# A two-layer graph network on one core: head 0's row sums split anew between TensorE, DMA and GpSimd, and a group's end copied in another order

## The chip, the cores and the metric

The kernel runs on one core of a Trainium2 chip. The metric is the device time of one execution in microseconds. Before the change it is 2827.12 us, the median of three runs (2824.92 to 2828.86). The engines are called TensorE (PE in the profile, PEld for its weight loads), VectorE (DVE), ScalarE (ACT), GpSimd (POOL) and SyncE (SP, which here only issues DMAs).

## The reference

Two layers, each in the form `x = x + layer(relu(layernorm(x)))`, over 4096 nodes with 512 features, all in float32. Layer 0 is a dense attention of one head. The change touches layer 1 alone, a graph attention with 8 heads of 64:

```python
data1 = (data @ W.T + b).reshape(N, H, D)            # N=4096, H=8, D=64
src = jnp.einsum('nhd,xhd->nh', data1, src_proj)
trg = jnp.einsum('nhd,xhd->nh', data1, trg_proj)
e = src.T[:, :, None] + trg.T[:, None, :]
e = jnp.where(e >= 0, e, 0.01 * e) + connectivity[None, :, :]
scores = jax.nn.softmax(e, axis=-1)
out = jnp.einsum('hnm,hmd->hnd', scores, data1.transpose(1, 0, 2))
```

Here `connectivity` is the matrix adj itself. For each head and each target row n, all 4096 sources m need a weight exp(leaky(src + trg) + adj), the weighted sum of the values, and the sum of the weights (the denominator).

## The kernel before, in words

**Work of layer 1.** The target rows come in 4 blocks of 1024 and the heads in 2 halves of 4, which makes 8 *groups*; a group walks over 32 *tiles* of 128 sources. So there are 256 steps. In each step the 128 sources lie on the partitions and the 1024 target rows in the free dimension, and four weight tiles of 128x1024, one per head (`pr[i, m, 0..3]`), are made and used.

**How the weights are made.** The exponential of the leaky sum is split into factors of the row, factors of the source and a maximum, so that one VectorE instruction makes a head's tile.
- ScalarE writes exp(adj) into PSUM (`exps`, L1085, one buffer, called `ex`). It writes exp(adj + a source's term) into SBUF (`last_exps`, L1095, `e3`).
- VectorE makes heads 3, 0, 1, 2 in this order (`weigh`, L1136 and L1133). Head 3's product takes `e3` and row factors, both in SBUF. The other three take `ex` from PSUM. `ex` can be written again when head 2's product has read it.
- Head 0 takes a relu of ScalarE first (`relus`, L1118). In every fourth tile (`BY_LOG`: 3, 7, ..., 31) head 0 goes another way: ScalarE writes a relu of the row terms (`logs`, L1101), GpSimd adds adj to it in two halves (`add_logs`, L1107), and ScalarE takes the exponential (L1115). VectorE then makes three products instead of four. The second half add is put behind head 3's product of the tile before, by an added dependency.

**What TensorE does** (`gather`). Per tile 16 value matmuls (L1171; 32 columns of weights, 512 columns moving) and 4 denominator matmuls (L1176, `dn<-pr,d_m`). Each matmul uses one of four 32-column strips of the array, so that four run side by side. Heads 1 and 2 get their denominators from those four matmuls. The denominators of heads 3 and 0 are gathered elsewhere:
- head 3: GpSimd adds each tile into one accumulator (`acc`, L1147, 128x1024);
- head 0: 24 tiles (`BY_DMA`) are added by accumulating DMAs, issued by GpSimd, into two accumulators in turn (L1154; tiles 0 and 1 are copied there, both at tile 1, L1152). The 8 other tiles (6, 10, 14, 18, 22, 26, 29, 31) go to TensorE as two further matmuls each (`dn<-pr,zo`), on strips 0 and 1 or 2 and 3 in turn (`side`).

In a group's last tile, TensorE sums the accumulators over the partitions by matmuls with a column of ones.

**A group's end.** In the last tile's step ScalarE copies the four value banks to SBUF (`os`, L1204). The denominators' bank (`dn`) is copied as `od` (L1210) in `finish`, after the next group's first step. The new group's tile 0 writes the same banks, so TensorE waits for these copies. `finish` runs in pieces, one at each step listed in `PARTS`: at step 1 products with `pick` (L1214), which bring the denominators to rows; at steps 2, 6, 10 and 14 two full-array transposes per row tile, behind the tile's matmuls (L1230); then scaling on ScalarE (L1257); at steps 5, 9, 13 and 17 a DMA from GpSimd that adds x (L1262); and at steps 8, 12, 16 and 18 the store from SyncE (L1260, L1265).

**Order of the work.** The order is written out by hand: each engine runs its instructions in the order of emission. In step s the functions of `stages` run for tiles ahead of s: loads 4 ahead, exponentials and products 1, factors 2, relus of the logs 4, TensorE 0. Then comes one piece of `finish`. Loads, broadcasts and stores share SyncE's queue; half adds, accumulations and their DMAs share GpSimd's. Buffers: `pr0` three, the other products two each, adj tiles four, `rl` two, `lg` one.

Of the kernel before, what the change touches and what calls it, by code (L numbers as in the profile page):

```python
# [15 lines left out]
P = 128  # L16
# [12 lines left out]
def kernel(  # L29
# [942 lines left out]
    zo = l1.tile([P, 3], FP, name="zo")  # L972

# [19 lines left out]

    PARTS = (0, 1, 2, 4, 5, 6, 8, 9, 10, 12, 13, 14, 16, 17, 18)
    BY_LOG = (3, 7, 11, 15, 19, 23, 27, 31)
    BY_DMA = [m for m in range(NT) if m not in (6, 10, 14, 18, 22, 26, 29, 31)]  # L1000
    after = mybir.DependencyInfo(mybir.DependencyClass.Sync, mybir.DependencyReason.DATA)

    with tc.tile_pool(name="p", bufs=2) as prp, tc.tile_pool(name="za", bufs=1) as zp0, tc.tile_pool(
# [17 lines left out]
        for t, val in ((d0_0, 0.0), (d0_m, 0.0), (zo[:, 0:2], 0.0), (zo[:, 2:3], 1.0)):  # L1021
            nc.gpsimd.memset(t, val)

        def tables():
# [26 lines left out]
        row = ident.rearrange("p (r s) -> p s r", s=Q)  # L1051
        nc.vector.tensor_copy(pick, row[:, 0:2, :])
        nc.vector.tensor_tensor(pick[:, 1, 0:HV], pick[:, 1, 0:HV], row[:, 2, HV:2 * HV], ALU.add)

        def zload(i, k):
            b, g = groups[i]
# [38 lines left out]
            nc.scalar.activation(x_, ra[i, m], AF.Exp, bias=ld_m[:, h // HG, m:m + 1])  # L1095
            e3[i, m] = x_

        def logs(i, m):
            if m in BY_LOG:
                r = rlp.tile([P, WL], FP, name="lg", bufs=1)  # L1100
                nc.scalar.activation(r, us[i], AF.Relu, bias=nlg_m[:, groups[i][1], m:m + 1], scale=-(1.0 - SLOPE))  # L1101
                rl[i, m] = r

        def add_logs(i, m, half, behind=None):
            if m in BY_LOG:
# [15 lines left out]
        def weigh(i, m, order=ORDER):  # L1121
            h = groups[i][1] * HG
            x_ = ex.pop((i, m))
            for k in order:
                if (i, m, k) in pr:
                    continue
                w = (prp if k else pr0p).tile([P, WL], FP, name=f"pr{k}")
                if k == 0 and (i, m) == (0, 0):
                    r = rlp.tile([P, WL], FP, name="rl")
                    nc.vector.tensor_scalar(r, zs_[0, 0], g_m[:, 0, 0:1], d_m[:, 0, 0:1], ALU.max, ALU.mult)  # L1130
                    nc.vector.tensor_tensor(w, r, x_, ALU.mult)
                elif k == 0:
                    nc.vector.scalar_tensor_tensor(w, rl.pop((i, m)), ngd_m[:, h // HG, m:m + 1], x_,  # L1133
                                                   op0=ALU.subtract, op1=ALU.mult)
                else:
                    p_ = nc.vector.scalar_tensor_tensor(w, zs_[i, k], g_m[:, h + k, m:m + 1],  # L1136
                                                        e3.pop((i, m)) if k == 3 else x_,
                                                        op0=ALU.max, op1=ALU.mult)
                    if k == 3:
                        add_logs(i, m + 1, 1, p_)  # L1140
                pr[i, m, k] = w
            w = pr[i, m, 3]
            if m == 1:
                acc[i, 3] = acp.tile([P, WL], FP, name="acc3", bufs=1)
                nc.gpsimd.tensor_tensor(acc[i, 3], pr[i, 0, 3], w, ALU.add)
            elif m > 1:
                nc.gpsimd.tensor_tensor(acc[i, 3], acc[i, 3], w, ALU.add)  # L1147
            add_logs(i, m + 2, 0)
            if m == 1:
                for n in range(2):  # L1150
                    acc[i, 0, n] = acp.tile([P, WL], FP, name=f"acc0{n}", bufs=1)
                    nc.gpsimd.dma_start(acc[i, 0, n], pr[i, n, 0])  # L1152
            elif m > 1 and m in BY_DMA:
                nc.gpsimd.dma_start(acc[i, 0, (len(BY_DMA) + BY_DMA.index(m)) % 2], pr[i, m, 0], accum_op=ALU.add)  # L1154

        def gather(i, m):
            b, g = groups[i]
# [2 lines left out]
                pv[i] = ([[p_v.tile([P, BL], FP, name=f"pv{c}{q}") for q in range(HV)] for c in range(2)],  # L1160
                         p_v.tile([P, BL], FP, name="dn"))
            v, dn = pv[i]
            by_pe = [u for u in range(NT) if u not in BY_DMA]
            side = sum(u < m for u in by_pe) % 2

            def values(c):
                for q in range(HV):
                    for r in (side, 1 - side):
                        k = ((3, 0), (1, 2))[c][r]
                        for c0 in range(0, D, Q):  # L1170
                            nc.tensor.matmul(v[c][q][r * D + c0:r * D + c0 + Q, :],  # L1171
                                             va[:, m, g * HG + k, c0:c0 + Q],
                                             pr[i, m, k][:, q * BL:(q + 1) * BL], start=(m == 0), stop=last)

            def den(r, w, src, q, **fl):
                nc.tensor.matmul(dn[r * Q:r * Q + w.shape[1], :], w, src[:, q * BL:(q + 1) * BL], **fl)  # L1176

            values(0)
            if last:
                for r, a in enumerate((acc[i, 0, 0], acc[i, 3])):  # L1180
                    for q in range(HV):
                        den(r * HV + q, zo[:, 1:3], a, q, start=False, stop=False)
                if m in by_pe:
                    for q in range(HV):
                        den(side * HV + q, zo[:, 1 - side:3], pr[i, m, 0], q, start=False, stop=False)
            values(1)
            for r in (side, 1 - side):
                for q in range(HV):
                    hk = g * 2 + r
                    den(r * HV + q, d0_m[:, hk, m, :] if m else d0_0[:, hk, :], pr[i, m, r + 1], q,  # L1190
                        start=(m == 0), stop=(last and r == 1))
            if m in by_pe and not last:
                for q in range(HV):
                    den(side * HV + q, zo[:, 1 - side:3], pr[i, m, 0], q, start=False, stop=False)
            if last:
                for q in range(HV):
                    den(q, zo[:, 1:3], acc[i, 0, 1], q, start=False, stop=True)
            for k in range(HG):
                pr.pop((i, m - 1, k), None)
            if last:  # L1200
                os_ = [[osp.tile([P, BL], FP, name=f"os{c}{q}") for q in range(HV)] for c in range(2)]
                for c in range(2):
                    for q in range(HV):
                        nc.scalar.copy(os_[c][q], v[c][q])  # L1204
                late[i] = os_, dn

        def denominators(i):
            os_, dn = late.pop(i)
            od = osp.tile([P, BL], FP, name="od")
            nc.scalar.copy(od, dn)  # L1210
            yield os_
            pd = p_t.tile([P, JT, 2, 4], FP, name="pt")
            for j in range(JT):
# [54 lines left out]
        def finish_last(i):  # L1268

            ys = [ep.tile([P, WT // 2, HG, D], FP, name="e") for _ in range(2)]  # L1270
            for n in range(2):
                nc.sync.dma_start(ys[n], part(x1, i, n * WT // 2, WT // 2))
            yield
            dens = denominators(i)
            os_ = next(dens)
            pts = []
# [68 lines left out]
        logs(0, 3)  # L1345
# [53 lines left out]
```

## Time and profile before

| | us |
|---|---|
| median of three runs | 2827.12 |
| profiled execution | 2827.62 |
| its span, first to last instruction | 2825.8 |
| layer 1, group 0 (1623.5 to 1771.2) | 147.7 |
| groups 1 to 6 | 150.0, 147.6, 148.1, 148.7, 147.5, 148.1 |
| group 7 and the kernel's end | 164.6 |

The profiled execution has 1.8 us around its span, and is 0.5 us over the median. A group is counted from the start of head 3's product of its tile 0. Layer 1 takes some 1200 us of the span. In a timeline a line has start, duration, engine, line and operation, what it writes and reads, and how many instructions it merges; brackets hold the engine's idle time before it and what ended that. A float32 matmul stands there as two instructions, so x8 is four matmuls.

### The profile page before, as it was taken

How to read it: one execution, taken by the hardware profiler on the slowest of the kernel's cores; microseconds unless marked ns; L12 is line 12 of the kernel's file. 1: busy time of each engine (PE TensorE's matmuls, PEld its weight loads, DVE VectorE, ACT ScalarE, POOL GpSimd, SP SyncE). 2: the span in 40 equal slices, each digit the busy share in tenths (PEclk: the TensorE clock that was granted, in tenths of full speed). 3: DMA queues.
4: the chain of work that ended last, by engine and by line, in shares of the span. 5: the costliest groups of instructions: out<-in, count | busy, mean ns of one | idle time of the engine just before them, and what ended most of it. 6: DMA issues, size and time to landing. Idle time of an engine off the chain costs nothing.

```text
span 2825.8 us, 46844 instructions
## 1 busy us (share of the span) xinstructions
PE 2757.8 (98%) x16843; PEld 1491.8 (53%) x16843; DVE 2508.6 (89%) x3425; ACT 1474.2 (52%) x2217; POOL 1397.6 (49%) x1178
## 2 busy tenths in 40 slices
PE   7999999998999999999999899999999999999998
PEld 4885444444888888888885323323232322232222
DVE  7877799898887888888886799999999999999998
ACT  2212233333123333433432188988788888888786
POOL 5323434444011010011106687887878787878786
PEclk9999999999999999999999999999999999999999
DMA  5637898987999999898877379989999898989896
GB/s 178 178 96 265 266 338 295 309 293 232 192 191 212 205 228 242 223 234 225 216 193 186 101 198 242 241 211 247 223 244 221 239 223 238 227 242 219 212 224 168
DMA packets 535992, 629.86 MB, mean 223 GB/s; under 512 B 292152, under 2 KB 346456, under 8 KB 535760
## 3 DMA queue, kind: packets, MB, share of 16 engines
q1 hardware_dynamic: 461920, 415.87, 49.6%
q0 software_dynamic: 71824, 207.07, 33.6%
q10 hardware_dynamic: 2016, 3.93, 0.4%
q8 instruction: 132, 2.16, 0.3%
q14 instruction: 100, 0.82, 0.1%
HBM read 404.23 MB, written 107.15 MB: 181 GB/s over the span
## 4 chain that ended last, share of the span: by engine, by line
PE 65%; DVE 13%; DMA 6%; issue 5%; ACT 4%; POOL 3%; SPq 2%; DVEq 0%; POOLq 0%; ACTq 0%
PE po L729 22%; PE pv L1171 15%; PE pe L525 12%; DVE pr L1136 8%; PE bank L267 6%; PE dn L1176 5%; PE po L863 4%; DMA acc<-pr 3%; SPq L656 2%; ACT e L1095 2%; DVE pr L1133 1%; POOL acc L1147 1%; DMA et<-er_d 1%; DVE mk L514 1%; DMA a<-in_adj_t_dram 1%
## 5 line engine op out<-in xcount | busy, mean ns | idle before, releaser
L1171 PE MATMUL pv<-pr,sup 128*32 128x512 f32 x8192 | 986.3, 594 | 13.8 <-POOL d L1342 10.2
L1147 POOL TENSOR_TENSOR acc<-acc,pr 128x1024 f32<-128x1024 f32 x240 | 576.5, 2402 | 146.9 <-DVE pr L1136 145.3
L1136 DVE SCALAR_TENSOR_TENSOR pr<-z,g_m,ex 128x1024 f32<-128x1024 f32 x512 | 630.4, 1270 | 2.9 <-ACT ex L1085 1.6
L1171 PEld LDWEIGHTS pv<-pr,sup 128*32 128x32 f32 x8192 | 282.6, 110 | 611.9 <-issue 547.1
L525 PE MATMUL pe<-he_t,he_t 128*128 128x512 f32 x896 | 387.9, 594 | 0.0
L690 ACT ACTIVATE d<-d 128x1024 f32<-128x1024 f32 x126 | 133.1, 1056 | 444.3 <-DVE d L682 237.9
L1136 DVE SCALAR_TENSOR_TENSOR pr<-z,g_m,e 128x1024 f32<-128x1024 f32 x256 | 345.2, 1348 | 3.2 <-PE pv L1171 3.2
L1085 ACT ACTIVATE ex<-e 128x1024 f32<-128x1024 f32 x256 | 263.3, 1029 | 144.8 <-DVE pr L1136 142.9
L1176 PE MATMUL dn<-pr,d_m 128*2 128x512 f32 x1984 | 318.5, 592 | 0.0
L1095 ACT ACTIVATE e<-e,ld_m 128x1024 f32<-128x1024 f32 x256 | 291.3, 1138 | 0.0
L525 PEld LDWEIGHTS pe<-he_t,he_t 128*128 128x128 f32 x896 | 169.8, 191 | 209.3 <-issue 193.7
L729 PE MATMUL po<-he_t,at 128*128 128x256 f32 x1024 | 263.8, 380 | 5.5 <-ACT he_t L740 5.5
L729 PE MATMUL po<-sup,u 128*128 128x256 f32 x1024 | 263.3, 380 | 0.0
L729 PE MATMUL po<-sup,at 128*128 128x256 f32 x1024 | 245.3, 383 | 8.3 <-DVE at L700 7.3
L1133 DVE SCALAR_TENSOR_TENSOR pr<-rl,ngd_m,ex 128x1024 f32<-128x1024 f32 x191 | 242.6, 1270 | 8.2 <-ACT ex L1085 8.2
L1118 ACT ACTIVATE rl<-z,ngd_m,d_m 128x1024 f32<-128x1024 f32 x191 | 234.7, 1229 | 0.0
L816 POOL DMA_DIRECT2D he_t<-he_t x56 | 48.9, 958 | 359.3 <-ACT he_t L732 304.3
L700 DVE TENSOR_TENSOR at<-d,a 128x1024 f32<-128x1024 f32 x126 | 154.0, 1223 | 77.2 <-PE po L729 45.8
L729 PEld LDWEIGHTS po<-sup,at 128*128 128x128 f32 x1024 | 196.3, 192 | 36.4 <-DVE at L700 8.1
L729 PEld LDWEIGHTS po<-he_t,at 128*128 128x128 f32 x1024 | 195.0, 191 | 32.4 <-issue 5.9
L729 PEld LDWEIGHTS po<-sup,u 128*128 128x128 f32 x1024 | 194.2, 190 | 26.2
L530 POOL DMA_DIRECT2D er_d<-mk x136 | 74.5, 548 | 237.8 <-DVE rm L527 226.4
(268 smaller groups left out, 3831.7 us busy)
## 6 DMA issues: line engine op xcount, KB each, us to landing
e<-in_adj_t_dram SPq DMA_DIRECT2D x256, 512.0 KB, 6.0
acc<-pr POOLq DMA_DIRECT2D x192, 512.0 KB, 6.2
a<-in_adj_t_dram SPq DMA_DIRECT2D x126, 512.0 KB, 5.2
ac<-in_adj_t_dram SPq DMA_DIRECT2D x124, 256.0 KB, 5.3
ar<-in_adj_dram SPq DMA_DIRECT2D x120, 256.0 KB, 5.0
ec_d<-mc POOLq DMA_DIRECT2D x120, 256.0 KB, 5.0
er_d<-mk POOLq DMA_DIRECT2D x112, 256.0 KB, 4.6
et<-er_d SPq DMA_DIRECT2D x448, 64.0 KB, 4.1
```

What stands on the lines that cost most here:

```text
L267: nc.tensor.matmul(acc[:, j, :], w, m, start=(k == 0), stop=(k == KC // 2 - 1))
L525: nc.tensor.matmul(pe[:, :w], he_t[i][:, k, (t % TB) * P:(t % TB + 1) * P], he_t[j][:, k, BL - w:], start=(k == 0), stop=(k == KC - 1))
L700: nc.vector.tensor_tensor(w, d, aj.pop((n, q)), ALU.mult)
L729: nc.tensor.matmul(acc[:, j, :], A[:, j * P:(j + 1) * P], B, start=(first_ and j == 0), stop=last, skip_group_check=True)
L1085: nc.scalar.activation(x_, ra.pop((i, m)), AF.Exp)
L1095: nc.scalar.activation(x_, ra[i, m], AF.Exp, bias=ld_m[:, h // HG, m:m + 1])
L1118: nc.scalar.activation(r, zs_[i, 0], AF.Relu, bias=ngd_m[:, h // HG, m:m + 1], scale=d_m[:, h, m:m + 1])
L1133: nc.vector.scalar_tensor_tensor(w, rl.pop((i, m)), ngd_m[:, h // HG, m:m + 1], x_, op0=ALU.subtract, op1=ALU.mult)
L1136: p_ = nc.vector.scalar_tensor_tensor(w, zs_[i, k], g_m[:, h + k, m:m + 1], e3.pop((i, m)) if k == 3 else x_, op0=ALU.max, op1=ALU.mult)
L1147: nc.gpsimd.tensor_tensor(acc[i, 3], acc[i, 3], w, ALU.add)
L1171: nc.tensor.matmul(v[c][q][r * D + c0:r * D + c0 + Q, :], va[:, m, g * HG + k, c0:c0 + Q], pr[i, m, k][:, q * BL:(q + 1) * BL], start=(m = ...
L1176: nc.tensor.matmul(dn[r * Q:r * Q + w.shape[1], :], w, src[:, q * BL:(q + 1) * BL], **fl)
```

## The change

In layer 1:
- **Head 0's sums.** Tiles 4, 8, ..., 28 (`BY_HALF`) are split: TensorE takes the first 512 target rows by one matmul, on strip 0, 1, 2, 3 in turn, and GpSimd adds the other 512 into a third accumulator `acc02`. Tile 31 goes to TensorE as two matmuls on strips 2 and 3. The other 24 tiles go by DMA: 6, 10, 14, 18, 22, 26 and 29 do now, and 4, 8, ..., 28 no longer. In the last tile there is one matmul more, for `acc02`.
- **Order of strips.** The matmuls of a tile start on the strip behind the last extra one (`cols`), instead of on one of two sides. `pick` adds three more rows for the new places, and `zo` has four columns.
- **Tile 0 at once.** The copies of tiles 0 and 1 into the accumulators are issued each at its own tile.
- **The first log.** The relu for tile 3 is made 5 tiles ahead instead of 4 (`early_logs`); the others stay.
- **A group's end.** In the last step only the first two value banks are copied. The other two and `dn` are copied in the next group's step 0 (`rest`), behind the exponential of tile 1. `od` is now a buffer of the pool of output tiles; its own is gone, and `acc02` takes as much.
- **PARTS.** The last store of a finished group is issued at step 21, not 18.

```diff
-    PARTS = (0, 1, 2, 4, 5, 6, 8, 9, 10, 12, 13, 14, 16, 17, 18)
+    PARTS = (0, 1, 2, 4, 5, 6, 8, 9, 10, 12, 13, 14, 16, 17, 21)
     BY_LOG = (3, 7, 11, 15, 19, 23, 27, 31)
-    BY_DMA = [m for m in range(NT) if m not in (6, 10, 14, 18, 22, 26, 29, 31)]
+    BY_HALF = (4, 8, 12, 16, 20, 24, 28)
+    BY_DMA = [m for m in range(NT - 1) if m not in BY_HALF]
...
+        for c in range(1, 4):
+            nc.vector.tensor_tensor(pick[:, 1, 0:1], pick[:, 1, 0:1], row[:, 3, c:c + 1], ALU.add)
...
-        def logs(i, m):
-            if m in BY_LOG:
+        def logs(i, m, early=False):
+            if m in BY_LOG and early == (m == BY_LOG[0]):
...
-            if m == 1:
-                for n in range(2):
-                    acc[i, 0, n] = acp.tile([P, WL], FP, name=f"acc0{n}", bufs=1)
-                    nc.gpsimd.dma_start(acc[i, 0, n], pr[i, n, 0])
-            elif m > 1 and m in BY_DMA:
+            if m < 2:
+                acc[i, 0, m] = acp.tile([P, WL], FP, name=f"acc0{m}", bufs=1)
+                nc.gpsimd.dma_start(acc[i, 0, m], pr[i, m, 0])
+            elif m in BY_DMA:
                 nc.gpsimd.dma_start(acc[i, 0, (len(BY_DMA) + BY_DMA.index(m)) % 2], pr[i, m, 0], accum_op=ALU.add)
+            if m == BY_HALF[0]:
+                acc[i, 0, 2] = acp.tile([P, BL], FP, name="acc02", bufs=1)
+                nc.gpsimd.tensor_copy(acc[i, 0, 2], pr[i, m, 0][:, BL:])
+            elif m in BY_HALF:
+                nc.gpsimd.tensor_tensor(acc[i, 0, 2], acc[i, 0, 2], pr[i, m, 0][:, BL:], ALU.add)
...
-            by_pe = [u for u in range(NT) if u not in BY_DMA]
-            side = sum(u < m for u in by_pe) % 2
+            n = sum(u < m for u in BY_HALF) % 4
+            cols = [(n + c) % 4 for c in range(4)]
...
+                for q in range(HV):
+                    ones(q, 1, halves(acc[i, 0, 0])[q])
+                for q in range(HV):
+                    ones(HV + q, 1, halves(acc[i, 3])[q])
+                ones(1, 1, acc[i, 0, 2])
+                for q in range(HV):
+                    ones(HV + q, 2, halves(pr[i, m, 0])[q])
             values(1)
...
+            if m in BY_HALF:
+                ones(n, 3 if n else 1, halves(pr[i, m, 0])[0])
...
-                for c in range(2):
-                    for q in range(HV):
-                        nc.scalar.copy(os_[c][q], v[c][q])
-                late[i] = os_, dn
+                for q in range(HV):
+                    nc.scalar.copy(os_[0][q], v[0][q])
+                late[i] = os_, v[1], dn
+
+        def rest(i, m):
+            if i and m == 0:
+                copy_rest(i - 1)
+
+        def copy_rest(i):
+            os_, v, dn = late[i]
+            for q in range(HV):
+                nc.scalar.copy(os_[1][q], v[q])
+            od = iop.tile([P, BL], FP, name="o")
+            nc.scalar.copy(od, dn)
+            late[i] = os_, od
...
-        stages = ((load, 4), (exps, 1), (weigh, 1), (factors, 2), (logs, 4), (scale, 2), (gather, 0))
+        stages = ((load, 4), (exps, 1), (rest, 0), (weigh, 1), (factors, 2), (logs, 4), (early_logs, 5), (scale, 2), (gather, 0))
```

More of the change, by code (lines that the diff above doesn't have):

```diff
@@ L1162, in gather @@
             v, dn = pv[i]
[L1163 to L1164 removed]
+            n = sum(u < m for u in BY_HALF) % 4
+            cols = [(n + c) % 4 for c in range(4)]
             def values(c):
                 for q in range(HV):
[L1168 removed]
+                    for col in cols:
+                        r, c0 = col // 2, col % 2 * Q
                         k = ((3, 0), (1, 2))[c][r]
[L1170 to L1173, printed above, removed]
@@ L1178, in gather, with ones, halves @@
+            def ones(col, row, src, stop=False):
+                den(col, zo[:, 3 - row:4], src, start=False, stop=stop)
+            def halves(src):
+                return [src[:, q * BL:(q + 1) * BL] for q in range(HV)]
             values(0)
             if last:
-                for r, a in enumerate((acc[i, 0, 0], acc[i, 3])):
-                    for q in range(HV):
[L1182 to L1185, printed above, removed]
```

36 lines of the change are left out of this document (18 added, 18 removed).

## The prediction, made before the change was run

> **What bounds the kernel now.** I read the page's first part, then busy time by group of layer 1 (one group runs from one start of tile 0 to the next), then the timelines of TensorE, ScalarE, VectorE and GpSimd at a group's end and around tiles 6 to 12.
>
> ```profile
> PE 2757.8 (98%) x16843; PEld 1491.8 (53%) x16843; DVE 2508.6 (89%) x3425; ACT 1474.2 (52%) x2217; POOL 1397.6 (49%) x1178
> 2365.60:2513.10 147.50, 146.42 (x1344) 43.57 (x1340) 145.28 (x122) 120.61 (x141) 117.22 (x76) 1.00 0.93 232
> ```
>
> The second line is group 5 (length; then PE, PEld, DVE, ACT, POOL busy): TensorE 146.4 and VectorE 145.3 of 147.5 us. Two engines are full at once, so relieving one is worth only what the other leaves.
>
> TensorE around the transposes of the finished group:
>
> ```profile
> 2106.43 1.04 PE L1176 MATMUL dn<-pr,d_m 128*2 128x512 f32 x8
> 2107.28 1.03 PE L1176 MATMUL dn<-pr,zo 128*2 128x512 f32 x4
> 2108.24 0.66 PE L1230 MATMUL pt<-ident,os 128*128 128x128 f32 x4
> 2108.83 3.64 PE L1171 MATMUL pv<-pr,sup 128*32 128x512 f32 x32
> 2113.14 3.62 PE L1171 MATMUL pv<-pr,sup 128*32 128x512 f32 x32
> 2117.44 3.62 PE L1171 MATMUL pv<-pr,sup 128*32 128x512 f32 x32
> ```
>
> A tile is 20 matmuls on four 32-column strips of the array. Tiles follow each other every 4.295 us, so a round of four matmuls side by side takes 0.859. Two extra matmuls (zo, half a round) ahead of a transpose, which needs all strips, cost a whole round: 2107.28 to 2108.24.
>
> The group's end on TensorE, ScalarE and VectorE:
>
> ```profile
> 2370.81 3.64 PE L1171 MATMUL pv<-pr,sup 128*32 128x512 f32 x32
> 2375.53 1.06 PE L1176 MATMUL dn<-pr,d 128*32 128x512 f32 x8 [1.08 <-ACT od L1210]
> ...
> 2367.69 1.23 ACT L1118 ACTIVATE rl<-z,ngd_m,d_m 128x1024 f32<-128x1024 f32 x1
> 2368.82 1.14 ACT L1101 ACTIVATE lg<-u,nlg_m 128x1024 f32<-128x1024 f32 x1
> 2369.86 2.02 ACT L1204 COPY os<-pv 128x512 f32<-128x512 f32 x4
> 2371.76 1.05 ACT L1085 ACTIVATE ex<-e 128x1024 f32<-128x1024 f32 x1
> 2374.89 0.58 ACT L1210 COPY od<-dn 128x512 f32<-128x512 f32 x1
> ...
> 2370.40 1.27 DVE L1136 SCALAR_TENSOR_TENSOR pr<-z,g_m,e 128x1024 f32<-128x1024 f32 x1
> 2372.84 1.28 DVE L1133 SCALAR_TENSOR_TENSOR pr<-rl,ngd_m,ex 128x1024 f32<-128x1024 f32 x1 [1.17 <-ACT ex L1085]
> ```
>
> The copies put the exponential late (VectorE idles 1.17) and od later still (TensorE loses 4.72 - 3.43 = 1.29 where four rounds of values lie).
>
> What GpSimd does to VectorE, the line I lean on most:
>
> ```profile
> 2102.84 1.20 POOL L1262 DMA_DIRECT2D o<-x  x1
> 2104.13 2.39 POOL L1147 TENSOR_TENSOR acc<-acc,pr 128x1024 f32<-128x1024 f32 x1
> 2106.28 1.33 DVE L1136 SCALAR_TENSOR_TENSOR pr<-z,g_m,e 128x1024 f32<-128x1024 f32 x1
> ...
> 2270.94 1.22 POOL L1262 DMA_DIRECT2D o<-x  x1 [1.86 <-DVE pr L1136]
> 2271.72 2.84 POOL L1147 TENSOR_TENSOR acc<-acc,pr 128x1024 f32<-128x1024 f32 x1
> 2273.38 2.28 DVE L1136 SCALAR_TENSOR_TENSOR pr<-z,g_m,e 128x1024 f32<-128x1024 f32 x1
> ```
>
> Head 3's product (pr<-z,g_m,e, both inputs in SBUF) ends 1.09 to 1.10 after a GpSimd add that it overlaps: 2106.52 to 2107.61, and 2274.56 to 2275.66, where the add was late. The head 0 to 2 products, which read PSUM, keep 1.27 beside the same adds.
>
> **The change part by part.** Profiled: span 2825.8, run 2827.62, 0.5 over the median 2827.12; the sum is made against 2827.62.
>
> *Matmuls.* Before, a group has 7 x 2 extra matmuls and in its last tile 8 more; after, 7 x 1 and 9. That is 22 - 16 = 6 fewer, on paper 1.5 rounds. But full-array matmuls stand after tiles 1, 2, 6, 10 and 14, and between two of them only the fullest strip counts. Tiles 3-6, 7-10, 11-14: 20 rounds plus two extras on two strips before, one extra on one strip after, 21 either way. From tile 15 to the next tile 1: 95 rounds, plus four per strip before; after, strip 1 still gets four (tile 24, acc00, acc02, acc01), the others three. So 167 rounds a group before and after: saved 0. Ends: 0 to 1.5 x 0.859 x 8 = 10.3 us; I take 0, by the zo and pt rows. The Trainium skill, TensorEngine Tiling (Array Packing), section Key Properties, calls tiles independent, by which six matmuls would be 1.5 rounds, 10.3 us; the next sentence there, that changing the tiling mode drains the array, is what the rows show. TensorE alone then needs 167 x 0.859 = 143.45, four transpose pairs at 0.72 (0.10 ahead of 2108.24, 0.59 to 2108.83, 0.03 in the tile behind) and 1.13 for the pick products at tile 1 (2380.81 to 2381.80, with the same drains): 147.46 a group when it never waits.
>
> *Group's end.* ScalarE's order is now relu, L1101, four os copies, L1085, L1095, relu, od; it becomes relu, two os copies, L1085, two os copies, od, L1095, relu, with L1101 (1.14) a tile earlier. od passes two activations (1.14 and 1.23), and both os copies behind L1085 are still done before TensorE wants their banks, 1.72 after the tile begins. TensorE's od stall (dn<-pr,d less four rounds: 1.30, 1.30, 0.23, 0.72, 1.26, 0.17, 0.74 over seven ends, 5.7 in all) goes. VectorE's 1.17 goes too. What is late next is the exponential of tile 0: L1101 now stands before it and takes 1.04 of ScalarE's queue where 0.38 was idle, so VectorE idles some 0.5 there. L1085 of tile 1 queues behind two copies that wait for TensorE's first half of the last tile (done by 2367), which is no new wait.
>
> *Half sums on GpSimd.* Seven adds of 128x512 at 1.28 (row L1107) per group. Behind acc (2.39) they end about 0.2 inside the next head 3's product, as L1107's first half does now; its tiles step 4.87 against 4.77. Price 0.10 x 7 = 0.7 of VectorE a group; ends 0 and 0.2 each.
>
> *DMAs moved to tiles 6, 10, 14, 18.* The decisive part. These tiles had no acc DMA; now they do (0.85 each), and there GpSimd also issues the output's accumulate (L1262, 1.22). Counted from the end of tile 6's head 3 product: half add 0.16 to 1.41, acc to 3.79, the new DMA to 4.64, L1262 to 5.86, acc of tile 7 to 8.25. Tile 8's head 3 product starts at 7.2 and would end at 8.52; by the 1.09 rule it ends at 9.34. So 0.82 of VectorE, four times a group, 3.3 us, in the seven groups with a finished one behind them. Ends: 0 (VectorE waits for TensorE's buffers there anyway) and 1.3 (another late 1.28 add in the way, as at 1879.59, where the product took 3.20). The Trainium skill, SBUF — State Buffer, section "SBUF: two separate sides", speaks against the change: the two engines share a port pair under an exclusive lock and the loser blocks for the whole instruction. Taken literally the product would run its 1.27 after 8.25 and lose 1.0, not 0.82; the rows give 1.09.
>
> *Rest.* Tile 0's copy at once: it waits for TensorE's last read of the old acc00 (2367.4 here) and for head 0's product (2368.1); behind it on GpSimd is only L1145 at 2371.81, with 6.0 idle before, so it is free. It removes ScalarE's waits for that landing (0.63 and 1.72 at L1115), which VectorE mostly did not see. Last output DMA at step 21 instead of 18: SP passes three loads ahead of it and no longer waits at it with them behind (head 3's product at 2468.18 took 1.70 after such a late load): 0.4 a group, which the pace below already lacks. od in the output pool: its slot is wanted again three outputs later, long free. Three 128x1 adds at the layer's start lie in the 4.6 us wait for z; without that, 3 us.
>
> *Sum.* VectorE's undisturbed pace is 18.08 for four tiles (head 3 products at 2343.88, 2347.50, 2352.32, 2357.09, 2361.96), so 8 x 18.08 = 144.6 a group, plus 0.7 + 3.3 + 0.5 and 0.1 for the reciprocal: 149.2. That is over TensorE's 147.5, so VectorE decides. Starts of dn<-pr,d (1781.14, 1931.19, 2078.80, 2226.89, 2375.53, 2523.07, 2671.18) give groups 2 to 6 now 148.0 in the mean: +1.2 for six groups (2 to 7), 7.2. Group 1 (150.05 now) has such collisions already, and a late load: -0.2. Group 0 has no finished group behind it: +0.7. Together +7.7: 2827.6 + 7.7 = 2835.
>
> **The rivals.**
> *VectorE absorbs it (20%).* If VectorE is far enough ahead to wait for buffers at tiles 7 and 8, the add has ended first and the collision vanishes; TensorE's 147.46 rules: (148.0 - 147.46) x 6 + 2.6 in group 1 = 5.8 gained, 2822. For it: such waits now stand at tiles 12 and 16 (2437.48, 0.16 <- PE dn). Against: none stands at tile 8, and VectorE has no lead left at a group's end: in group 4 tile 30's last product ends at 2362.04 and TensorE wants it at 2362.2 (1.72 into its tile). It decides from about 0.6 of lead more at tile 7.
> *The collision costs more (12%).* At 1.3 each, and the adds behind it late in turn: 4 x 0.48 x 7 = 13 on top, 2848.
> *The six matmuls do count (5%).* Then 10.3 + 5.7 go: 2811. Against: the transposes' row, and VectorE's pace.
> *The change does nothing (5%).* Each collision is half absorbed, 0.41: 2835 - 28 x 0.41 = 2823.5, at most 2830.
>
> **How the numbers follow.** Forecast 58%. Its own range is 2828 to 2842 (0.57 to 1.07 a collision, 28 of them: -7 and +7). The range is stretched to 2820 for the first rival and to 2843 for the foot of the second; outside lie two thirds of the second, the third, and the edges: about 18%. A measurement tells 0.2%, 5.7 us, from no change: 2821.5 to 2832.8. Forecast: 44 slower, 14 same. First rival: 12 faster, 8 same. Second: 12 slower. Third: 5 faster. Rest: 2 faster, 1 same, 2 slower. Faster 0.19, same 0.23, slower 0.58.
>
> **What would show it.** Right: head 3's products of tiles 8, 12, 16, 20 at about 2.1 us, dn<-pr,d without an od wait, TensorE waiting for pr in tiles 24 to 30, groups of 149 us, L1262 straight behind an acc DMA. Wrong: those products at 1.3 and groups at 147.5 (first rival), or 2.5 and more (second); transposes that start less than 0.86 after a single extra matmul (third).

## The result, and the profile after

The changed kernel takes 2834.49 us (median of 15 runs, 2828.43 to 2837.49); in the same sets of runs the kernel before takes 2827.50 (15 runs). The ratio is 1.0022, with a 95% interval of 1.0014 to 1.0030: some 6 us slower. The profiled execution took 2831.62 us, with a span of 2829.7.

| start to start of head 3's first product, us | before | after |
|---|---|---|
| layer 1 begins at | 1623.56 | 1620.36 |
| group 0 | 147.6 | 148.7 |
| group 1 | 150.0 | 149.7 |
| groups 2 to 6 | 147.6, 148.1, 148.6, 147.5, 148.1 | 149.1, 149.0, 149.1, 149.0, 149.1 |
| group 7 and the kernel's end | 164.6 | 165.6 |
| layer 1 in all | 1202.3 | 1209.3 |

Layer 1 is 7.1 us longer, which is what the medians say. The two spans differ by 3.9 only, because layer 0, which the change does not touch, was 3.2 us shorter in this execution. Groups 2 to 6 no longer differ in length.

Busy time and the chain of waits of the page after:

```profile
PE 2764.7 (98%) x16747; PEld 1524.5 (54%) x16747; DVE 2525.5 (89%) x3428; ACT 1475.6 (52%) x2217; POOL 1463.3 (52%) x1234
...
PE 51%; DVE 27%; issue 9%; ACT 5%; DMA 4%; SPq 2%; POOL 2%; DVEq 0%; ACTq 0%; POOLq 0%
```

TensorE has 48 matmuls (96 instructions) fewer and is busier all the same. Its busy time here is not a measure of work: the same 8192 instructions of the value matmuls are busy for 1050.4 us instead of 986.3, with a mean of 594 ns in both pages. VectorE's share of the chain is 27%; in the profile before it was 13%. The same move shows in busy time over group 5 (length; then PE, PEld, DVE, ACT, POOL busy with instruction counts; clock; DMA share; GB/s):

```profile
2365.95:2514.98 149.03, 148.67 (x1344) 48.16 (x1340) 148.32 (x123) 120.72 (x142) 125.68 (x83) 1.00 0.93 230
```

VectorE is busy for all but 0.7 of 149.0 us; before it was 145.3 of 147.5. Where those 3 us come from, in VectorE's groups of instructions (count, busy us, mean ns, idle time before them; the first line is the profile before, the others the one after):

```profile
L1136 DVE SCALAR_TENSOR_TENSOR pr<-z,g_m,e 128x1024 f32<-128x1024 f32 x256 | 345.2, 1348 | 3.2 <-PE pv L1171 3.2
...
L1142 DVE SCALAR_TENSOR_TENSOR pr<-z,g_m,ex 128x1024 f32<-128x1024 f32 x512 | 630.1, 1269 | 1.9 <-PE dn L1186 1.7
L1142 DVE SCALAR_TENSOR_TENSOR pr<-z,g_m,e 128x1024 f32<-128x1024 f32 x256 | 364.2, 1423 | 0.0
L1139 DVE SCALAR_TENSOR_TENSOR pr<-rl,ngd_m,ex 128x1024 f32<-128x1024 f32 x191 | 242.4, 1269 | 2.7 <-ACT ex L1088 2.7
```

Only head 3's product (pr<-z,g_m,e) has changed its duration: 1423 ns in the mean, 1348 before. The other two lines have 1269, and 1270 before. One of the slow ones, tile 20 of group 5, with GpSimd's queue first and VectorE's behind it, in the timeline:

```profile
2453.87 2.38 POOL L1153 TENSOR_TENSOR acc<-acc,pr 128x1024 f32<-128x1024 f32 x1
2456.20 0.86 POOL L1159 DMA_DIRECT2D acc<-pr  x1
2456.78 1.52 POOL L1287 DMA_DIRECT2D o<-x  x1
2457.52 3.19 POOL L1153 TENSOR_TENSOR acc<-acc,pr 128x1024 f32<-128x1024 f32 x1
...
2456.02 1.30 DVE L1142 SCALAR_TENSOR_TENSOR pr<-z,g_m,e 128x1024 f32<-128x1024 f32 x1
2457.25 2.46 DVE L1142 SCALAR_TENSOR_TENSOR pr<-z,g_m,ex 128x1024 f32<-128x1024 f32 x2
2459.64 2.17 DVE L1142 SCALAR_TENSOR_TENSOR pr<-z,g_m,e 128x1024 f32<-128x1024 f32 x1
```

Head 0's DMA and the output's DMA stand behind each other at tile 18; the add of tile 19 therefore ends at 2460.71, and the product of tile 20, which began at 2459.64, ends at 2461.81, 1.10 after it. (GpSimd's rows overlap, since an instruction's record begins while the one ahead still runs; the ends count.) VectorE does not idle here, it is held inside an instruction, so no view of waits names this. In tile 7 of the same group VectorE also waits for a buffer that TensorE still reads:

```profile
2400.67 2.47 DVE L1142 SCALAR_TENSOR_TENSOR pr<-z,g_m,ex 128x1024 f32<-128x1024 f32 x2 [0.27 <-PE dn L1186]
```

What TensorE does near the end of the same group's VectorE-bound stretch, tiles 24 to 26, in the timeline:

```profile
2481.92 3.59 PE L1181 MATMUL pv<-pr,sup 128*32 128x512 f32 x28
...
2486.34 4.04 PE L1181 MATMUL pv<-pr,sup 128*32 128x512 f32 x32
2490.20 1.04 PE L1186 MATMUL dn<-pr,d_m 128*2 128x512 f32 x8
2491.05 1.90 PE L1181 MATMUL pv<-pr,sup 128*32 128x512 f32 x16
2493.32 1.92 PE L1181 MATMUL pv<-pr,sup 128*32 128x512 f32 x16 [0.36 <-DVE pr L1142]
```

Sixteen value matmuls take 3.62 when nothing is late; here it is 4.04, and then a wait for VectorE's product by name. And the group's end, TensorE first, then ScalarE:

```profile
2374.72 0.61 PE L1186 MATMUL dn<-pr,d 128*32 128x512 f32 x3
...
2365.60 1.13 ACT L1104 ACTIVATE lg<-u,nlg_m 128x1024 f32<-128x1024 f32 x1
2366.64 1.01 ACT L1088 ACTIVATE ex<-e 128x1024 f32<-128x1024 f32 x1
...
2369.76 1.04 ACT L1219 COPY os<-pv 128x512 f32<-128x512 f32 x2
2371.38 1.03 ACT L1088 ACTIVATE ex<-e 128x1024 f32<-128x1024 f32 x1 [0.58 <-DVE pr L1142]
2372.34 1.06 ACT L1229 COPY os<-pv 128x512 f32<-128x512 f32 x2
2373.29 0.60 ACT L1231 COPY o<-dn 128x512 f32<-128x512 f32 x1
```

The denominators' copy begins at 2373.29, before TensorE wants the bank, and dn<-pr,d has no wait in brackets. The exponential of tile 1 no longer stands behind four copies; it waits for VectorE. The relu L1104 now stands ahead of tile 0's exponential.

### The profile page after: what moved, and what is told of

Same layout as the page of the kernel before. It is cut to its first block, busy times and chain, and to the rows that moved or that the text cites. A ratio compares the mean times of both kernels' runs of the same rounds, so it can differ in the third digit from the quotient of the medians.

```text
span 2829.7 us, 46758 instructions
## 1 busy us (share of the span) xinstructions
PE 2764.7 (98%) x16747; PEld 1524.5 (54%) x16747; DVE 2525.5 (89%) x3428; ACT 1475.6 (52%) x2217; POOL 1463.3 (52%) x1234
## 4 chain that ended last, share of the span: by engine, by line
PE 51%; DVE 27%; issue 9%; ACT 5%; DMA 4%; SPq 2%; POOL 2%; DVEq 0%; ACTq 0%; POOLq 0%
PE po L729 23%; DVE pr L1142 18%; PE pe L525 12%; PE bank L267 6%; DVE pr L1139 4%; PE pv L1181 4%; PE po L863 4%; ACT e L1098 2%; SPq L656 2%; PE dn L1186 1%; DMA et<-er_d 1%; ACT rl L1124 1%; DMA acc<-pr 1%; DVE mk L514 1%; POOL lg L1113 1%
## 5 line engine op out<-in xcount | busy, mean ns | idle before, releaser
L1181 PE MATMUL pv<-pr,sup 128*32 128x512 f32 x8192 | 1050.4, 594 | 16.6 <-POOL d L1368 10.4
L1153 POOL TENSOR_TENSOR acc<-acc,pr 128x1024 f32<-128x1024 f32 x240 | 594.6, 2477 | 109.8 <-DVE pr L1142 108.8
L1181 PEld LDWEIGHTS pv<-pr,sup 128*32 128x32 f32 x8192 | 322.6, 110 | 595.2 <-issue 491.7
L1142 DVE SCALAR_TENSOR_TENSOR pr<-z,g_m,ex 128x1024 f32<-128x1024 f32 x512 | 630.1, 1269 | 1.9 <-PE dn L1186 1.7
L1186 PE MATMUL dn<-pr,d_m 128*2 128x512 f32 x1984 | 370.4, 592 | 0.0
L1142 DVE SCALAR_TENSOR_TENSOR pr<-z,g_m,e 128x1024 f32<-128x1024 f32 x256 | 364.2, 1423 | 0.0
L1139 DVE SCALAR_TENSOR_TENSOR pr<-rl,ngd_m,ex 128x1024 f32<-128x1024 f32 x191 | 242.4, 1269 | 2.7 <-ACT ex L1088 2.7
```

Of the source, the lines that this page charges most:

```text
L1181: nc.tensor.matmul(v[c][q][col * Q:(col + 1) * Q, :], va[:, m, g * HG + k, c0:c0 + Q], pr[i, m, k][:, q * BL:(q + 1) * BL], start=(m == 0) ...
L1186: nc.tensor.matmul(dn[col * Q:col * Q + w.shape[1], :], w, src, **fl)
```

## The experiments

Each set of runs has its own runs of the kernel before, whose median lay between 2827.5 and 2832.5, so kernels of different sets are compared by their ratio to it. *Group* is the mean length of groups 3 to 6 in the profiled execution, counted as above.

| kernel | median, before's in its set | ratio, 95% interval | group |
|---|---|---|---|
| before | | | 148.10 |
| the change | 2834.49, 2827.50 | 1.0022 (1.0014 to 1.0030) | 149.04 |
| output's DMAs two tiles on | 2838.76, 2832.52 | 1.0026 (1.0017 to 1.0034) | 148.76 |
| the same, acc02 on strip 3 | 2837.92, 2832.52 | 1.0020 (1.0011 to 1.0029) | 148.78 |
| before, other tiles by TensorE | 2843.03, 2832.52 | 1.0045 (1.0031 to 1.0058) | 150.13 |
| before, new group's end | 2830.27, 2832.52 | 0.9996 (0.9986 to 1.0006) | 147.86 |
| the change without half adds | 2835.72, 2831.13 | 1.0010 (1.0000 to 1.0021) | 148.53 |
| eight tiles by TensorE | 2822.75, 2831.13 | 0.9967 (0.9956 to 0.9978) | 147.34 |
| six tiles by TensorE | 2818.76, 2831.13 | 0.9947 (0.9932 to 0.9962) | 146.49 |
| six tiles, strips uneven | 2823.88, 2831.13 | 0.9971 (0.9955 to 0.9986) | 147.31 |
| before, store at step 21 | 2824.68, 2828.54 | 0.9987 (0.9979 to 0.9996) | 147.67 |
| the change without the output's DMA | 2822.33, 2828.54 | 0.9977 (0.9969 to 0.9986) | 147.29 |
| drains a tile earlier | 2811.24, 2828.54 | 0.9941 (0.9929 to 0.9953) | 145.66 |

**The collision, taken away.**

```diff
-                nc.gpsimd.dma_start(o, part(x1, i, t, 2), accum_op=ALU.add)
```

> The changed kernel without the output's accumulating DMA from GpSimd (1.22 of its queue, four times a group), so that x is not added to the output of seven groups: that part of the work is left out. Collision theory: head 3's products of tiles 8, 12, 16, 20 fall from 1.7 to 2.1 us to some 1.3, VectorE needs 145.9 a group, TensorE's 147.3 rules, groups of 147.3 to 147.7 instead of 149.05: 10 to 12 us less than the changed kernel, 3 to 6 less than before. Rival, that the acc DMA ahead or the half sums make those products late: they stay above 1.7, and the time stays.

Measured: ratio 0.9977 where the change has 1.0022, which is 0.45% or 12.7 us, a little over the 10 to 12 expected; by the medians 6.2 us less than before. The groups have the expected 147.3. Tile 20 of group 5 again, GpSimd first, then VectorE:

```profile
2452.71 2.39 POOL L1153 TENSOR_TENSOR acc<-acc,pr 128x1024 f32<-128x1024 f32 x1 [0.43 <-DVE pr L1142]
2455.06 0.84 POOL L1159 DMA_DIRECT2D acc<-pr  x1
...
2455.11 1.28 DVE L1142 SCALAR_TENSOR_TENSOR pr<-z,g_m,e 128x1024 f32<-128x1024 f32 x1
```

The add of tile 19 ends at 2455.10, as the product begins, and the product takes 1.28. So 1.2 us of GpSimd's queue, four times a group, is what makes VectorE the bound. The half sums are still in this kernel and the acc DMAs stand where the change put them; neither holds the product up alone. The run takes the output's transfer away together with its issue. That the issue is what counts is read from the timelines: with it, the add behind the issue ends late, and the product ends 1.10 after that add.

**The collision, added alone to the kernel before.**

```diff
-    BY_DMA = [m for m in range(NT) if m not in (6, 10, 14, 18, 22, 26, 29, 31)]
+    BY_DMA = [m for m in range(NT) if m not in (4, 8, 12, 16, 20, 24, 28, 31)]
```

> The kernel before with one edit: tiles 4, 8, ..., 28 and 31 go to TensorE as two matmuls instead of 6, 10, 14, 18, 22, 26, 29 and 31, so that tiles 6, 10, 14, 18 get a DMA of head 0 ahead of the output's DMA. Nothing else of the change. Collision theory: head 3's products of tiles 8, 12, 16, 20 at about 2.1 us, VectorE 144.6 + 3.3 + 1.2 at the group's end = 149.1 a group, 2835 (2831 to 2840), as slow as the whole change. Rival, that the collision is absorbed and the loss is from the other parts: 2825 to 2829.

Measured: 1.0045, 10.5 us over the kernel before, groups of 150.1. The direction and the products of tiles 12, 16 and 20 are as the theory has them (2.12 to 2.16 in groups 2 to 7, 1.87 to 1.90 at tile 8), and the size is toward the upper end of the 3 to 12 us that the expected range gives: here a second delay counts in full. Group 5 in the timeline: head 3's product of tile 20, then the half add of the logs that is late, and the product of tile 23:

```profile
2467.51 2.16 DVE L1136 SCALAR_TENSOR_TENSOR pr<-z,g_m,e 128x1024 f32<-128x1024 f32 x1
...
2478.12 2.24 POOL L1107 TENSOR_TENSOR lg<-lg,e 128x512 f32<-128x512 f32 x1 [1.14 <-DMA e<-in_adj_t_dram]
...
2482.71 3.21 DVE L1136 SCALAR_TENSOR_TENSOR pr<-z,g_m,e 128x1024 f32<-128x1024 f32 x1
```

The half add waits 1.14 for a load, which SyncE issues behind the store at step 18; GpSimd's adds behind it are late in turn, and the product takes 3.21. The whole change moves this store to step 21. With VectorE as the bound it costs 0.7 to 1.8 a group (tiles 22 and 23 step 5.55 to 5.76 and 3.6, or 4.77 and 5.51, instead of 4.87 and 3.62). This is one reason why the change as a whole is less slow than its DMA move alone.

**The output's DMAs moved out of the way.**

```diff
-    PARTS = (0, 1, 2, 4, 5, 6, 8, 9, 10, 12, 13, 14, 16, 17, 21)
+    PARTS = (0, 1, 2, 4, 7, 8, 10, 11, 12, 14, 15, 16, 18, 19, 23)
```

> The changed kernel, with the pieces of a finished group two steps later: the output's accumulating DMAs fall in the steps that weigh tiles 8, 12, 16 and 20, which have no DMA of head 0, and no longer behind one in tiles 6, 10, 14 and 18. Collision theory: head 3's products of tiles 8, 12, 16, 20 fall from 1.7 to 2.1 us to 1.3 to 1.4, VectorE needs 145.9 a group, TensorE's 147.5 rules, groups of 147.5 to 147.8 instead of 149.1; seven groups, with 2.1 for group 1: 11 us less than the changed kernel, 2823.5 (2820 to 2826). Rival, that the half sums and the new order at a group's end are what costs: no change, 2834.

A miss: 1.0026, no better than the change. Around tile 14 of group 5, GpSimd first, then VectorE:

```profile
2435.87 1.21 POOL L1287 DMA_DIRECT2D o<-x  x1 [0.71 <-ACT o L1282]
2436.66 2.84 POOL L1153 TENSOR_TENSOR acc<-acc,pr 128x1024 f32<-128x1024 f32 x1
2439.02 1.71 POOL L1113 TENSOR_TENSOR lg<-lg,e 128x512 f32<-128x512 f32 x1
...
2440.10 1.71 DVE L1142 SCALAR_TENSOR_TENSOR pr<-z,g_m,e 128x1024 f32<-128x1024 f32 x1
```

The DMA waits there for the output's scaling; the add and the half add of the logs are late in turn, the latter ends at 2440.73, and the product of tile 14 ends 1.08 after it. In this group tiles 12 to 15 step 5.09, 4.97, 5.21 and 3.61 (18.88), against 5.66, 4.87, 4.86 and 3.62 (19.01) at tiles 20 to 23 of the change and 18.16 at its tiles 24 to 27, where nothing collides. The collision moved by two tiles and lost a sixth of its price; group 1 lost 2.5 more, with VectorE waiting 4.5 for ScalarE's exponential. The expectation had left out that GpSimd's queue has no gap to move to: four tiles there hold four adds (2.39 each), two half adds of the logs and one half sum (1.28 each), three DMAs of 0.85 and one of 1.22, together 17.2 of 18.2.

With one matmul on another strip in addition:

```diff
-                ones(1, 1, acc[i, 0, 2])
+                ones(3, 2, acc[i, 0, 2])
```

> The kernel with the output's DMAs two tiles on, and in the last tile the matmul for acc02 on strip 3 (row 2) instead of strip 1 (row 1): the same number of matmuls, but from tile 17 to the next tile 1 the strips then have 3, 3, 3, 3 extra ones instead of 3, 4, 3, 2. Theory that the fullest strip counts: one round of 0.86 less in each of 8 groups, 6.9 us less than the kernel with the DMAs moved alone, some 2817, as VectorE's 145.9 lies below TensorE's 146.6. Rival, that the number of matmuls counts: no difference between the two.

The groups are the same (148.78 and 148.76). As VectorE bounds both kernels, this says nothing on the strips; they come up again further down, where TensorE is the bound.

**The half sums.** Of this block only the copy of tile 4 stays:

```diff
-            elif m in BY_HALF:
-                nc.gpsimd.tensor_tensor(acc[i, 0, 2], acc[i, 0, 2], pr[i, m, 0][:, BL:], ALU.add)
```

> The changed kernel without GpSimd's half adds of tiles 8, 12, ..., 28 (tile 4's copy stays), so that 512 target rows lack these tiles in head 0's sums: their work is left out, nothing takes its place. Theory (0.10 of VectorE per half add, VectorE decides): 6 x 0.10 x 8 = 4.8 us less than the changed kernel, which is then still 3 over the kernel before. Rivals: nothing, if it is hidden; 10 and more, if the half adds also push the adds that collide.

Measured: 1.0010 against 1.0022, 3.4 us, with intervals that overlap. The lengths are clearer: layer 1 has 1205.1 instead of 1209.3, where 4.8 was expected. The steps of tiles 9, 13, ..., 29 are 4.77, and 4.87 in the change: 0.10 each. The price stands.

**The group's end alone.** The kernel before with `rest`, `copy_rest` and `early_logs` of the change:

```diff
-                for c in range(2):
-                    for q in range(HV):
-                        nc.scalar.copy(os_[c][q], v[c][q])
-                late[i] = os_, dn
+                for q in range(HV):
+                    nc.scalar.copy(os_[0][q], v[0][q])
+                late[i] = os_, v[1], dn
...
-        stages = ((load, 4), (exps, 1), (weigh, 1), (factors, 2), (logs, 4), (scale, 2), (gather, 0))
+        stages = ((load, 4), (exps, 1), (rest, 0), (weigh, 1), (factors, 2), (logs, 4), (early_logs, 5), (scale, 2), (gather, 0))
```

> The kernel before with the new order at a group's end alone: two value banks copied in the last tile, the other two and dn behind the exponential of the next tile 1, and the relu of tile 3 a tile earlier. Theory: TensorE's waits for od (5.7 us over seven ends) and VectorE's 1.17 at tile 1 go, against 0.5 at tile 0; TensorE's 147.5 rules where the mean is 148.0: 3 to 6 us gained, 2822 to 2825. Rival, that the wait only changes place (VectorE late at tile 0): 2827 to 2829.

Measured: 0.9996. The interval runs from 4.0 us gained to 1.7 lost, so no gain is shown, and of the 3 to 6 us expected only the lower end is left. (Layer 1 of the profiled execution is 3.5 shorter.) Something new is late, at tiles 2 and 3 of group 6: GpSimd, ScalarE and VectorE in the timeline.

```profile
2531.95 0.88 POOL L1157 DMA_DIRECT2D acc<-pr  x1 [0.89 <-DMA acc<-pr]
...
2531.57 1.15 ACT L1118 ACTIVATE pr<-lg,t_m 128x1024 f32<-128x1024 f32 x1 [3.37 <-PE pt L1226]
...
2533.66 2.47 DVE L1139 SCALAR_TENSOR_TENSOR pr<-z,g_m,ex 128x1024 f32<-128x1024 f32 x2 [1.51 <-ACT ex L1085]
```

With tiles 0 and 1 both copied at tile 1, tile 0's weights leave their buffer late. ScalarE's log exponential of tile 3 writes that buffer (`pr0` has three), and it is held for 3.37 until about the time at which GpSimd's DMA of tile 2, which needs the same copy, is let go. The profile names another releaser here; over the whole kernel it puts 31.3 us of this instruction's waits down to the DMA acc<-pr, 24.5 in the kernel before, and none in the change, where tile 0 is copied at once. Tile 3's step is 3.87 to 5.47 in groups 2 to 7 of this kernel, 3.87 to 3.95 before (where VectorE had just lost its 1.17 at tile 1) and 3.86 or 3.87 in the change. The store at step 18 takes as much again: tiles 22 and 23 together have 9.1 to 10.2 in these groups, 8.8 to 9.4 in the kernel before. Summed over groups 2 to 7, tile 3 loses 3.0 against 3.87, and tiles 22 and 23 lose 3.1 against the kernel before.

**The whole change without its new split.** The group's end, tile 0 at once and the store at step 21, with the eight tiles of the kernel before:

```diff
+            if m < 2:
+                acc[i, 0, m] = acp.tile([P, WL], FP, name=f"acc0{m}", bufs=1)
+                nc.gpsimd.dma_start(acc[i, 0, m], pr[i, m, 0])
+            elif m in BY_DMA:
...
+    PARTS = (0, 1, 2, 4, 5, 6, 8, 9, 10, 12, 13, 14, 16, 17, 21)
```

> The kernel before with the change's order at a group's end, tile 0 copied at once and the last store at step 21; head 0's sums as before, eight tiles by TensorE. Theory: no collision is added, TensorE's 147.46 a group rules instead of 148.3 in the mean of groups 1 to 6: 7 x 0.9 = 6 us less than before (4 to 8, ratio 0.9972 to 0.9986), 3 less than with the new order at the group's end alone. Rival, that a late store and late copy cost nothing: no more than the new order at the group's end alone, 2 us less than before.

Measured: 0.9967, 8.4 us by the medians, a little over the 4 to 8 expected; layer 1 of the profiled execution is 5.9 shorter. The store alone, in the kernel before:

```diff
-    PARTS = (0, 1, 2, 4, 5, 6, 8, 9, 10, 12, 13, 14, 16, 17, 18)
+    PARTS = (0, 1, 2, 4, 5, 6, 8, 9, 10, 12, 13, 14, 16, 17, 21)
```

> The kernel before with the last store of a finished group at step 21 instead of 18, and nothing else. Theory: the loads behind it on SyncE are no longer late, tiles 22 and 23 step 4.87 and 3.62 instead of up to 5.5 and 3.9; 0.4 a group, 3 us in seven groups (1 to 4), as TensorE's waits for od stay. Rival: VectorE's late start there is made good by TensorE's lead, no change.

Measured: 0.9987, 3.9 us, as expected (1 to 4; layer 1 is 3.6 shorter); tiles 22 and 23 step 4.87 and 3.62. So the parts of the change beside the split are worth 8 us by the medians, and the new split costs 15; by the lengths of layer 1 it is 6 and 13.

**Strips.** In the kernel with eight tiles and all other parts of the change TensorE sets the pace, so from there its rounds can be counted. Six tiles by TensorE instead of eight:

```diff
-    BY_DMA = [m for m in range(NT) if m not in (6, 10, 14, 18, 22, 26, 29, 31)]
+    BY_DMA = [m for m in range(NT) if m not in (6, 10, 14, 18, 22, 31)]
```

> The kernel before with the change's order at a group's end, tile 0 copied at once and the last store at step 21, but head 0's sums as before: tiles 6, 10, 14, 18, 22 and 31 to TensorE as two matmuls each, tiles 26 and 29 now by DMA. No DMA of head 0 is ahead of the output's DMA, and no half adds. From tile 15 to the next tile 1 the strips have 3, 3, 3, 3 extra matmuls instead of 4, 4, 4, 4. TensorE 147.46 - 0.86 = 146.6 a group, VectorE 144.6 + 0.5 + 0.1 = 145.2: groups of 146.6 to 147.0 against 148.3 in the mean before, 7 x 1.5 and the round of group 0: 10 to 13 us less than before (ratio 0.9955 to 0.9965). Rival, that VectorE's order decides and TensorE's rounds don't: 4 to 6 us less, as much as with eight tiles.

and the same with two matmuls of tile 31 put on the other strips:

```diff
-            side = sum(u < m for u in by_pe) % 2
+            side = 0 if last else sum(u < m for u in by_pe) % 2
```

> The kernel of six tiles by TensorE with one edit: tile 31's two matmuls on strips 0 and 1 instead of 2 and 3, so that from tile 15 to the next tile 1 the strips have 4, 4, 2, 2 extra matmuls instead of 3, 3, 3, 3. The number of matmuls is the same. Theory that the fullest strip counts: one round of 0.86 more in each of 8 groups, 6.9 us more than with even strips. Rival, that the number of matmuls counts: no difference.

Busy time over group 5 of the kernels with eight tiles, six tiles, and six tiles on uneven strips:

```profile
2368.99:2516.33 147.34, 147.34 (x1352) 44.28 (x1348) 145.31 (x122) 120.69 (x142) 117.25 (x76) 1.00 0.92 233
```

```profile
2363.38:2509.92 146.54, 146.54 (x1344) 43.95 (x1340) 145.82 (x122) 120.41 (x142) 119.04 (x78) 1.00 0.96 241
```

```profile
2362.31:2509.64 147.33, 147.33 (x1344) 43.75 (x1340) 145.26 (x123) 120.67 (x142) 118.90 (x78) 1.00 0.96 240
```

Six tiles by TensorE are 12.4 us faster than the kernel before by the medians, where 10 to 13 was expected (the ratio, 0.9947, is a little under the 0.9955 to 0.9965 given for it); a group is 0.85 shorter than with eight, about one round. With the same 1344 instructions the uneven strips cost 0.8 a group (0.82 in the mean of groups 3 to 6; 5.1 us in the medians and 6.4 in layer 1, where 6.9 was expected; the two ratios' intervals overlap slightly), and the group is then as long as with 1352. So the fullest strip counts, not the number of matmuls. The edit also lets the values of the last tile start on the other two strips; that this order costs nothing by itself is not shown. The Trainium skill, TensorEngine Tiling (Array Packing), section Key Properties, says both that tiles operate independently and that a change of mode drains the array. The runs fit the two together: from drain to drain the fullest strip sets the time.

The last run moves the drains. The transposes stand behind tiles 2, 5, 9 and 13, and the matmuls of tiles 6 and 9 share a stretch on opposite strips:

```diff
-    PARTS = (0, 1, 2, 4, 5, 6, 8, 9, 10, 12, 13, 14, 16, 17, 21)
+    PARTS = (0, 1, 2, 4, 5, 8, 9, 12, 13, 16, 17, 21)
-    BY_DMA = [m for m in range(NT) if m not in (6, 10, 14, 18, 22, 31)]
+    BY_DMA = [m for m in range(NT) if m not in (6, 9, 10, 14, 18, 31)]
...
-                    if j == 0:
-                        if t:
-                            nc.sync.dma_start(part(out, i, t - 2, 2), old)
-                        yield
+                if t:
+                    nc.sync.dma_start(part(out, i, t - 2, 2), old)
+                yield
                 nc.gpsimd.dma_start(o, part(x1, i, t, 2), accum_op=ALU.add)
                 old = o
-                yield
+            yield
```

> The kernel of six tiles by TensorE with the transposes behind tiles 2, 5, 9 and 13 instead of 2, 6, 10 and 14 (both halves of an output scaled in one step for it), and tiles 6, 9, 10, 14, 18, 31 by TensorE: as many matmuls and DMAs. Between two drains the extra rounds are then 0 (tiles 3 to 5), 1 (6 to 9, two tiles on opposite strips), 1 (10 to 13) and 3 (14 to the end), 5 instead of 6. Drain theory: TensorE 0.86 a group less, 145.6, against VectorE's 145.2 and some more for ScalarE's longer step: groups of 145.7 to 146.3 instead of 146.4, 1 to 5 us less than with six tiles, 0.2% at most. Rival: as the number of matmuls is the same, no gain, or a loss of 2 to 6 by VectorE's wait for an exponential behind the scaling.

Measured: 2811.24 us, 0.9941, the fastest kernel here; groups of 145.66. A drain of the kernel with six tiles, and one of this kernel, on TensorE:

```profile
2399.82 1.04 PE L1178 MATMUL dn<-pr,d_m 128*2 128x512 f32 x8
2400.67 1.03 PE L1178 MATMUL dn<-pr,zo 128*2 128x512 f32 x4
2401.63 0.66 PE L1241 MATMUL pt<-ident,os 128*128 128x128 f32 x4
```

```profile
2386.67 1.04 PE L1178 MATMUL dn<-pr,d_m 128*2 128x512 f32 x8
2387.64 0.66 PE L1241 MATMUL pt<-ident,os 128*128 128x128 f32 x4
```

From the last denominators to the transpose it is 1.81 with two extra matmuls on two strips and 0.97 without: 0.84 for half a round of work. The gain over six tiles is 0.83 a group, where 0.1 to 0.7 was expected; that the totals differ by more than chance is not shown, as the ratios' intervals overlap. Nor is the drain the only thing that moved: the output's DMAs stand elsewhere too, and in groups 2 to 7 no product of head 3 takes more than 1.41 here, while the six-tile kernel has six between 1.68 and 2.82. In group 3, where neither kernel has such a product, the gain is 0.84 (145.65 against 146.49). Busy time over group 5 shows TensorE and VectorE both full (145.70 and 145.21 of 145.70):

```profile
2354.52:2500.22 145.70, 145.70 (x1344) 43.89 (x1340) 145.21 (x122) 120.40 (x142) 118.86 (x78) 1.00 0.97 243
```

## Why the prediction was right

Forecast was 2835 (2820 to 2843), 7.7 us more than the profiled execution before; measured were 2834.49, with layer 1 7.1 us longer. The mechanism is the forecast one: VectorE decides, held by late adds of GpSimd, and TensorE's six matmuls save nothing. That the total came within 0.5 us is partly luck: single runs of the changed kernel lie 9 us apart, and a group 0 that was 0.4 over its forecast set off part of the 0.1 to 0.2 by which the other groups were under theirs.

- *Matmuls: 0 saved.* In the changed kernel it can't be seen, since VectorE decides. Where TensorE decides it holds: the uneven strips cost a round with no matmul more. TensorE alone was put at 147.46 a group with 167 rounds; the eight-tile kernel has 147.34, and the change without the output's DMA 147.29, though it has six matmuls fewer a group. By the same count of the fullest strip the uneven six-tile kernel has 167 rounds, the even one 166 and the one with other drains 165, so estimates of 147.46, 146.60 and 145.74 at 0.859 a round; measured were 147.31, 146.49 and 145.66. Counted by matmuls these three would be equal.
- *The group's end.* TensorE's od wait and VectorE's 1.17 are gone (tile 1 steps 4.77 instead of 6.03). Tile 0 steps 5.30 instead of 4.82: 0.48, forecast 0.5.
- *Half sums: 0.10 each.* 4.87 against 4.77; the run without six of them gives 0.10 each again. There are six adds, not the seven of the sum: tile 4's is a copy of 0.60, and tile 5 steps 4.77 as before. So 0.6 a group, forecast 0.7.
- *DMAs moved: 0.82 a collision, 3.3 a group.* In group 5 tiles 8, 12, 16 and 20 step 0.44, 0.70, 0.82 and 0.84 longer than 4.82. The rest stands at tiles 7 and 11 (3.96 and 3.74 instead of 3.62), where VectorE waits for TensorE's buffer: together 3.3. In group 1, where VectorE has next to no such wait, all four products take 2.04 to 2.08, and their steps alone are 3.0 longer in sum. So the rival in which such a wait absorbs the collision was there in part (the product of tile 8 takes 1.76, not 2.1), but it saves nothing: the add ends when it ends, the product 1.1 behind it, and a wait ahead only takes the place of the lengthening. Taking the DMA away and adding the collision alone both confirm the step.
- *Rest.* The store was priced well (0.4 a group; 3.9 us in the run alone). Wrong was "free" for tile 0's copy, in two ways: the prediction has it that VectorE mostly did not see the waits which it removes. That was true with the old group's end only. With the new one and both copies at tile 1 VectorE loses up to 1.6 at tile 3, so by this reading the small edit lets the new end pay; no run has it alone. In group 0 it is not free either: the first add of GpSimd comes 7.7 us after the group's start instead of 7.0 with the new end alone, behind that DMA, head 3's product of tile 2 takes 2.09 instead of 1.38, and tiles 2 and 3 together take 9.81 instead of 9.28. That is about what group 0 came out over its forecast.
- *Sum.* 149.2 a group forecast, 149.04 measured in groups 2 to 6. Group 1 came out 0.3 shorter (forecast 0.2), group 0 1.1 longer (forecast 0.7).

The other rivals of the prediction stood on sizes that the runs now bound: the collision costs neither 1.3 nor half of 0.82, and the six matmuls do not count.

## What to carry to other kernels

Before work is moved from one engine to another, write down the queue of the helper over a few tiles, issues of DMAs included: here 1.2 us of issue on GpSimd pushed an add into the one product of VectorE that it held up, and no view of waits shows that, since VectorE counts as busy. Compare an instruction's mean duration by its inputs between two profiles to find such a hold. And where small matmuls run on strips, count rounds between drains by the fullest strip, and place both the drains and the extras with that count; here the groups became some 0.8 us shorter with each round that it took out.

## What the runs showed of the hardware that was not expected

- The hold has one size whatever causes it: head 3's product ended 1.08 to 1.10 after the GpSimd add that it met, for a 128x1024 add (2460.71 to 2461.81) as for a 128x512 half add (2440.73 to 2441.81), with 1.07 of overlap in the first case and 0.63 in the second. In the thirteen traces head 3's product began 2355 times with 0.2 us or more of such an add still to run, and ended 1.08 to 1.11 after the add in all but five cases (1.26 to 1.29, all in group 0). No product of heads 0 to 2 of the same form took more than 1.29 in any of them. The Trainium skill, SBUF — State Buffer, section "SBUF: two separate sides", says that whichever of the two starts first has the shared ports for its whole instruction, and that the other fully blocks. Taken literally, that would put the product's full 1.27 behind the add, 0.17 to 0.19 more than measured.
- A small cost became a larger one when the bound moved: behind the store at step 18, tiles 22 and 23 take 0.3 to 0.9 longer in groups 2 to 7 of the kernel before, and 0.7 to 1.8 with the collisions added, where VectorE has no lead.
- The start of layer 1 lay between 1620.4 and 1632.0 us in the thirteen profiled executions, with layer 0 the same in all. That is more than most effects here, so single spans can't be compared at this size; lengths of groups and ratios of many runs can.
